# Expert rows turned by VectorE and transfers, second product one tile later, first products before the last routing

## The chip, the core and the metric

The kernel runs on one core of a Trainium2 chip, as one launch. A core has TensorE (PE: matrix products; PEld is its loading of weights), VectorE (DVE), ScalarE (ACT), GpSimd (POOL) and SyncE (SP), which run their instruction queues side by side and wait for one another by semaphores, and 16 DMA engines. The metric is the device time of one execution in microseconds (us). It is given as the median of several runs; a profile is one further execution with the hardware profiler.

## What is computed

The input is 4 sequences of 512 tokens of 512 features, all in f32. Two layers follow, each with an attention-like part and a feed-forward part, both gated and added to the stream. Layer 0 (quantised products with each sequence's own weights, then a ternary feed-forward) and the 16-head cross attention of layer 1 are not touched in what they compute. What the change is about is the last part, a mixture of experts:

```python
router_in = norm_w * (xf * rsqrt(mean(xf * xf) + EPS))
probs = softmax(router_in @ router_w.T)
topw, topi = top_k(probs, 2);  topw = topw / sum(topw)
cw = zeros((T, 8)).at[arange(T)[:, None], topi].add(topw)
a = silu(einsum('td,edf->tef', flat, gate_w)) * einsum('td,edf->tef', flat, up_w)
y = einsum('ted,te->td', einsum('tef,efd->ted', a, down_w), cw) * 4
x = x + tanh(g_ffn[1]) * y        # flat = layernorm(x), 2048 tokens, 8 experts of width 256
```

The kernel computes only the two chosen experts of each token.

## The kernel before, in words

**Attention and what lies beside it.** The 64 heads (16 for each of 4 sequences; LAST is 64) run in a pipelined loop. In one iteration `ask` makes the queries of the next head, `weigh` the scores and softmax of this one (its weights are turned by VectorE in 32x32 blocks, L513, and 16 small transfers, L527, of 64 KB each), `take` multiplies the values of an earlier one (L635) and copies the product to `oT` (ACT, L639), and `add` projects a still earlier one (L649). The last head's 16 transfers are issued from two queues, SP and ACT. A list `beside` holds generators that are advanced by one or two steps an iteration (`step_beside`): the routing of each finished sequence and a sort.

**Routing and sorting.** `route(b)` normalises a sequence, puts its rows (with their eight weights, 520 floats a row) into the table `xtab` in DRAM, and picks two experts for every token (L707 to L790; the products with the router are L748). `sort` gives every token a seat so that the tokens of one expert stand together: 39 tiles of 128 rows, 16 of them (sort a) from the first three sequences, 23 (sort b) from what remains. For each of 24 or 32 columns of tokens it makes one comparison row `in_row` (L905) and two halves of `in_seg` (L907), all on VectorE, and TensorE multiplies them (L912) into the list of row numbers `ids`. Sort b needs the routing of the last sequence, which comes after attention.

**Experts.** The gate and up weights (`gu`) and down weights (`dn`) of all eight experts lie in SBUF. One tile goes through these steps: `gather` (POOL, an indirect transfer of 128 rows, L1021, into one of four buffers `xg`; VectorE picks the tile's weight `cwj`, L1024 and L1025); `expert_in`: four transposes of the rows on TensorE (L1033), a copy to `xgT` by VectorE (L1035), four products with the gate and up weights (L1038; an f32 product runs in two passes, so eight matmuls), Silu on ACT (L1042) and the gating multiply on VectorE (L1043); `expert_out`: two transposes of the hidden values (L1051), a copy to `hidT` (L1053), two products with the down weights (L1056, four matmuls), a copy `y` on ACT (L1060, three buffers), and an indirect scatter-add into the output in DRAM (POOL, L1061). Two tiles may add to one token, so each scatter-add waits until the one before has landed; a dependency written out by hand says so. `expert_out` of a tile is called after `expert_in` of the next one.

**What sets the order.** The program is written in a framework that schedules the instructions of each engine into one fixed order and inserts the waits; pools with a number of buffers decide how far work may run ahead. An engine executes its queue strictly in that order, so an instruction that waits holds all that stands behind it on the same engine, transfers that the engine issues included. In the expert loop gathers run up to three tiles ahead, and from tile 13 on the rest of `beside` (sort b) is run out first.

Of the kernel before, what the change touches and what calls it, by code (L numbers as in the profile page):

```python
# [32 lines left out]
NHEAD, NKV, HD = 16, 8, 128  # L33
# [8 lines left out]
NE, TOPK, FE = 8, 2, 256  # L42
NF = FE // P
# [4 lines left out]
NSEG = (TOK * TOPK + NE * (P - 1)) // P  # L48
NA, TA = 16, 12
NB = NSEG - NA  # L50
ROW = D + NE
# [5 lines left out]
def kernel(  # L57
# [30 lines left out]
    ident = cp.tile([P, P], F32, name="ident")  # L88
# [8 lines left out]
    gu = wp.tile([P, NE, KD, 2 * FE], F32, name="gu")  # L97
    dn = wp.tile([P, NE, NF, D], F32, name="dn")
# [31 lines left out]
    def acc_tile():  # L130
        return acc_p.tile([P, 512], F32, tag="acc", name="acc")
# [68 lines left out]
    with tc.tile_pool(name="q8", bufs=1) as q8, tc.tile_pool(name="l0", bufs=2) as l0, tc.tile_pool(  # L200
        name="w0", bufs=1
# [291 lines left out]
        for b in range(B):  # L493
            xT = ternary_in(b)
# [4 lines left out]
            keys_values(b, lambda: bank(3), load_context(b, nc.sync))  # L499


    l1_ctx = ctx.enter_context(ExitStack())

    la = l1_ctx.enter_context(tc.tile_pool(name="la", bufs=2, reuse_waits="tile"))
    l1 = l1_ctx.enter_context(tc.tile_pool(name="l1", bufs=2, reuse_waits="tile"))

    NQ, Q = P // 32, 32
# [64 lines left out]
        nc.vector.tensor_reduce(seen[b], u8, AX.X, ALU.max)  # L572

    def load_queries(n):
        th = la.tile([P, KD, HD], F32, tag="wq", name="wq")
# [131 lines left out]
    def route(b, pool):  # L707
# [5 lines left out]
        if b + 1 < B:  # L713
            xn, xT, blocks = gu[:, 4], spare_xT if b % 2 == 0 else homes[b], turn_blocks()
        else:
            xn = pool.tile([P, NT, D], F32, name="xnl")
            xT = pool.tile([P, NQ, KD, P], F32, name="xTl")
            blocks = None
        ss = small(NT, "ss")
        for t in range(NT):  # L720
            norm(t, xn[:, t, :D])
            if blocks is not None:
                turn_tile_apart(xn[:, t, :D], blocks, t)
            else:
                tp = work_tile()
                for i in range(KD):
                    nc.tensor.transpose(tp[:, i * P : (i + 1) * P], xn[:, t, i * P : (i + 1) * P], ident)
                evacuate(
                    xT.rearrange("p a k q -> p (a k q)").rearrange("p (q k t) -> p t k q", k=KD, t=NT)[:, t],
                    tp.rearrange("p (k q) -> p k q", k=KD),  # L730
                )
            sq = gu[:, 5, 2 + t % 2, :] if b + 1 < B else pool.tile([P, D], F32, tag="sq", name="sq", bufs=2)
# [12 lines left out]
        for t in range(NT):  # L745
            ps = work_tile()
# [96 lines left out]
    def sort(pool, part, nt, c0, n, spans):  # L843
# [52 lines left out]
        yield  # L896

        if c0:
            in_row = pool.tile([P, TOPK * nt, P], BF16, name="in_row")
        else:  # L900
            in_row = place_in(gu, 5 * SLOT, TOPK * nt * P // 2).bitcast(BF16).rearrange("p (i q) -> p i q", q=P)
        in_seg = pool.tile([P, TOPK * nt, 2, n], BF16, name=part + "in_seg", bufs=1)
        for i in range(TOPK * nt):
            s, t = divmod(i, nt)
            nc.vector.tensor_scalar(in_row[:, i, :], col, lo[:, s, t : t + 1], None, ALU.is_equal)  # L905
            for u, v in enumerate((row1[:, 0:1], float(P * t))):
                nc.vector.tensor_scalar(in_seg[:, i, u, :], cols, hi[:, s, t : t + 1], v, ALU.is_equal, ALU.mult)  # L907
            if i % 8 == 7:
                yield
        ps = work_tile()  # L910
        for i in range(TOPK * nt):
# [65 lines left out]


    loads = {NHEAD + e: [(load_dn, e)] for e in range(NE)}
    for i, e in ((24, 6), (30, 0), (48, 7), (44, 1), (57, 2), (60, 4), (62, 3), (63, 5)):  # L980
        loads[i] = [(load_gu, e)]

    for _ in queries_in(0):
        pass
# [3 lines left out]
    for i in range(LAST + 3):  # L988
        b, n = divmod(i, NHEAD)
        if i == 2:  # L990
            router_constants()
        if n == NHEAD - 6 and b + 1 < B:
            beside.insert(0, queries_in(b + 1))
        if i + 1 < LAST:
            ask(i + 1)
        load_head(i + 2)
        if 2 <= i < LAST + 2:
            wos[i - 2] = load_out((i - 2) % NHEAD)
        if i < LAST:
            weigh(i)  # L1000
        for load, e in loads.get(i, ()):
            load(e)
        if i >= 3:
            add(i - 3)
        if 2 <= i < LAST + 2:
            take(i - 2)
        step_beside()
        if b == B - 1:
            step_beside()
    while beside:  # L1010
        step_beside()


    l1_ctx.close()
    mo = ctx.enter_context(tc.tile_pool(name="moe", bufs=1, reuse_waits="tile"))

    def gather(j):
        ids, _, owned = found[j]
        xg = mo.tile([P, ROW], F32, tag="xg", name="xg", bufs=4)
        table = xtab[: TA * P, :] if j < NA else xtab[:, :]  # L1020
        nc.gpsimd.indirect_dma_start(xg, None, table, bass.IndirectOffsetOnAxis(ap=ids, axis=0))  # L1021
        cwj = small(1, "cwj")
        junk = small(NE, "junk")
        nc.vector.tensor_tensor(junk, xg[:, D:], owned, ALU.mult)  # L1024
        nc.vector.tensor_reduce(cwj, junk, AX.X, ALU.add)  # L1025
        return xg, cwj

    def expert_in(j, xg, cwj):

        e = nc.tensor.value_load(found[j][1], min_val=0, max_val=NE - 1)  # L1030
        tp = work_tile()
        for k in range(KD):
            nc.tensor.transpose(tp[:, k * P : (k + 1) * P], xg[:, k * P : (k + 1) * P], ident)  # L1033
        xgT = mo.tile([P, KD * P], F32, tag="xgT", name="xgT", bufs=2)
        nc.vector.tensor_copy(xgT, tp)  # L1035
        ps = acc_tile()
        for k in range(KD):
            nc.tensor.matmul(  # L1038
                ps, lhsT=xgT[:, k * P : (k + 1) * P], rhs=gu[:, bass.ds(e, 1), k, :], start=(k == 0), stop=(k == KD - 1)
            )  # L1040
        h = mo.tile([P, FE], F32, tag="hid", name="hid", bufs=2)
        nc.scalar.activation(h, ps[:, :FE], AF.Silu)  # L1042
        nc.vector.scalar_tensor_tensor(h, h, cwj, ps[:, FE:], ALU.mult, ALU.mult)  # L1043
        return e, h

    written = []

    def expert_out(j, e, h):
        tp = work_tile()
        for f in range(NF):  # L1050
            nc.tensor.transpose(tp[:, f * P : (f + 1) * P], h[:, f * P : (f + 1) * P], ident)  # L1051
        hT = mo.tile([P, NF * P], F32, tag="hidT", name="hidT", bufs=2)
        nc.vector.tensor_copy(hT, tp[:, : NF * P])  # L1053
        ps = acc_tile()
        for f in range(NF):
            nc.tensor.matmul(  # L1056
                ps, lhsT=hT[:, f * P : (f + 1) * P], rhs=dn[:, bass.ds(e, 1), f, :], start=(f == 0), stop=(f == NF - 1)
            )
        y = mo.tile([P, D], F32, tag="y", name="y", bufs=3)
        nc.scalar.copy(y, ps)  # L1060
        add = nc.gpsimd.indirect_dma_start(  # L1061
            yacc,
            bass.IndirectOffsetOnAxis(ap=found[j][0], axis=0),
            y,
            None,
            bounds_check=TOK - 1,
            oob_is_err=False,
            compute_op=ALU.add,
        )
# [12 lines left out]
    got = {}  # L1082
    pending = None
    for j in range(NSEG):
        if j >= NA - 3:
            while beside:
                step_beside()
        for i in range(j, min(j + 3, NSEG)):
            if i not in got and i in found:
                got[i] = gather(i)  # L1090
        e, h = expert_in(j, *got[j])
        if pending is not None:
            expert_out(*pending)
        pending = (j, e, h)
        step_beside()
    expert_out(*pending)


# [33 lines left out]
```

## Time and profile before

| | |
|---|---|
| runs | 1644.98, 1646.61, 1650.31 us; median 1646.61 us |
| profiled execution | 1646.0 us, span of its records 1644.2 us |
| TensorE | busy 1535.6 us, mean granted clock 0.978 |
| VectorE, ACT, POOL busy | 924.0, 565.8, 442.3 us |
| attention ends, experts begin (first L1033 on TensorE) | 1376.38 us |
| last scatter-add starts | 1638.23 us |
| gather (L1021), mean on POOL | 1.0 us, 35 of them after 1375 us |
| scatter-add (L1061), mean on POOL | 1.58 us, 39 of them |
| scatter-add to its landing, median | 4.8 us |
| moved in 1500 to 1550 us | 80 GB/s; in 1300 to 1350 us (attention) 139 GB/s |

How to read it: a timeline line has the start, the busy time, engine, line, operation and tiles of a run of equal instructions, and in brackets the idle time of the engine just before and the instruction that ended it. In the slices of the page, each digit is the busy share of one fortieth of the span in tenths, and PEclk the clock that TensorE was granted. An issue line of a DMA ends with the median time from issue to landing.

### The profile page before, as it was taken

What the parts mean: (1) busy time and instruction counts of PE and PEld (TensorE: products, weight loads), DVE (VectorE), ACT (ScalarE), POOL (GpSimd) and SP (SyncE); (2) the same over time, 40 slices, a digit from 0 to 9 for tenths busy, and PEclk for the clock granted to TensorE, in tenths of its full rate; (3) what the DMA queues carried; (4) which work ended last, traced back from release to release, by engine and by line L of the source; (5) the groups of instructions that cost most, each with busy time, mean ns of one, the idle gap of its engine ahead of it and who ended that gap; (6) DMA issues with size and microseconds to landing.
All of it is one profiled execution on the core that took longest, in us unless ns stands there. A gap on an engine that the chain in (4) does not pass through costs nothing. (4 is left out here: it accounts for less than half of the span.)

```text
span 1644.2 us, 16560 instructions
## 1 busy us (share of the span) xinstructions
PE 1535.6 (93%) x4524; PEld 771.9 (47%) x4524; DVE 924.0 (56%) x2478; ACT 565.8 (34%) x1180; POOL 442.3 (27%) x549
## 2 busy tenths in 40 slices
PE   4786888999999999999999999999999988999997
PEld 2443655676434444445444445444454434544443
DVE  5567777662155555585665764555768553372221
ACT  2645453633333333352333442333522322211111
POOL 1155433432211113131131130131311102334442
PEclk9898999999999999999999998999999998999999
DMA  8552100113445556576455674575756453444341
GB/s 304 194 184 73 65 20 32 46 52 90 141 137 152 145 135 159 135 202 163 106 160 135 165 190 110 136 184 134 212 149 160 130 144 108 77 79 83 73 79 25
DMA packets 109771, 208.26 MB, mean 127 GB/s; under 512 B 28193, under 2 KB 32289, under 8 KB 109681
## 3 DMA queue, kind: packets, MB, share of 16 engines
q0 software_dynamic: 30896, 88.57, 21.7%
q1 hardware_dynamic: 66960, 96.54, 21.6%
q10 hardware_dynamic: 11824, 22.09, 4.0%
q8 instruction: 39, 0.64, 0.2%
q14 instruction: 52, 0.42, 0.1%
HBM read 98.76 MB, written 35.72 MB: 82 GB/s over the span
## 5 line engine op out<-in xcount | busy, mean ns | idle before, releaser
L615 DVE CUSTOM_DVE_ANT_0 e<-bank,mask_b 128x512 f32<-128x512 f32 x256 | 174.9, 688 | 261.4 <-PE bank L610 261.2
L649 PE MATMUL acc<-wo,oT 128*128 128x512 f32 x512 | 235.5, 603 | 4.1 <-ACT oT L639 4.1
L635 PE MATMUL bank<-eT,v 128*128 128x512 f32 x512 | 230.5, 593 | 2.9 <-DMA eT<-blocks 1.7
L610 PE MATMUL bank<-kT,qT 128*128 128x512 f32 x512 | 232.3, 593 | 0.7 <-ACT dn L458 0.7
L618 ACT ACTIVATE e<-e,nmax 128x512 f32<-128x512 f32 x256 | 184.3, 720 | 95.5 <-DVE nmax L615 88.6
L597 PE MATMUL bank<-gu,wq 128*128 128x512 f32 x384 | 178.3, 601 | 2.3 <-DVE nmax L615 2.3
L513 DVE STREAM_TRANSPOSE blocks<-e 128x512 f32<-128x512 f32 x256 | 158.9, 677 | 21.5 <-DMA eT<-blocks 17.5
L649 PEld LDWEIGHTS acc<-wo,oT 128*128 128x128 f32 x512 | 98.8, 194 | 129.7 <-issue 121.9
L635 PEld LDWEIGHTS bank<-eT,v 128*128 128x128 f32 x512 | 97.1, 190 | 126.0 <-issue 112.0
L610 PEld LDWEIGHTS bank<-kT,qT 128*128 128x128 f32 x512 | 97.0, 190 | 124.8 <-issue 114.5
L1038 PE MATMUL acc<-gu,xgT 128*128 x312 | 143.3, 603 | 4.7 <-issue 3.2
L639 ACT COPY oT<-bank 128x512 f32<-128x512 f32 x64 | 37.4, 584 | 306.7 <-PE bank L635 289.7
L576 POOL DMA_DIRECT2D wq<-in_L_xattn_Wq_dram x64 | 48.5, 757 | 264.0 <-PE bank L597 251.8
L597 PEld LDWEIGHTS bank<-gu,wq 128*128 128x128 f32 x384 | 73.0, 192 | 92.9 <-issue 80.5
L591 POOL DMA_DIRECT2D wo<-in_L_xattn_Wo_dram x64 | 36.8, 575 | 270.3 <-PE acc L649 262.6
L626 DVE TENSOR_SCALAR e<-e,rt 128x512 f32<-128x512 f32 x256 | 108.0, 484 | 2.1
L601 ACT ACTIVATE qT<-bank 128x512 f32<-128x512 f32 x64 | 38.2, 597 | 171.8 <-PE bank L597 166.1
L1038 PEld LDWEIGHTS acc<-gu,xgT 128*128 128x128 f32 x312 | 59.9, 194 | 78.8 <-issue 78.3
L405 PE MATMUL acc<-pjT,hT 128*128 128x512 f32 x320 | 87.2, 402 | 5.7 <-DVE hT L430 5.7
L418 PE MATMUL bank<-xfT,fcT 128*128 128x512 f32 x320 | 87.4, 404 | 0.0
L1056 PE MATMUL acc<-dn,hidT 128*128 x156 | 75.8, 608 | 6.0 <-DVE hidT L1053 5.6
L405 PEld LDWEIGHTS acc<-pjT,hT 128*128 128x128 f32 x320 | 59.2, 188 | 19.4 <-DVE hT L430 7.3
(329 smaller groups left out, 1970.8 us busy)
## 6 DMA issues: line engine op xcount, KB each, us to landing
eT<-blocks SPq DMA_DIRECT2D x1016, 64.0 KB, 2.8
wq<-in_L_xattn_Wq_dram POOLq DMA_DIRECT2D x64, 256.0 KB, 4.1
wo<-in_L_xattn_Wo_dram POOLq DMA_DIRECT2D x64, 256.0 KB, 3.1
kd<-dn SPq DMA_DIRECT2D x32, 256.0 KB, 2.4
vd<-dn SPq DMA_DIRECT2D x32, 256.0 KB, 2.0
kT<-kd POOLq DMA_DIRECT2D x32, 256.0 KB, 3.6
v<-vd POOLq DMA_DIRECT2D x32, 256.0 KB, 4.2
stage<-in_L_ffn_w_fc_dram ACTq DMA_DIRECT2D x20, 256.0 KB, 3.0
```

Of the source, the lines that this page charges most:

```text
L405: nc.tensor.matmul(outs[t], lhsT=h[:, t * P : (t + 1) * P], rhs=pjT[:, j, :], start=(j == 0 and u == 0), stop=(j == NH - 1 and u == 1),)
L418: nc.tensor.matmul(ps, lhsT=fcT[:, i, j * P : (j + 1) * P], rhs=xT[u][:, i, :], start=(u == 0 and i == 0), stop=(u == 1 and i == KD - 1),)
L513: nc.vector.transpose(blocks[:, :, :, t, :].rearrange("p c s r -> p s c r"), src.rearrange("p (s c i) -> p s c i", c=NQ, i=Q))
L597: nc.tensor.matmul(ps, lhsT=th[:, i, :], rhs=xT[:, :, i, :], start=(i == 0), stop=(i == KD - 1))
L610: nc.tensor.matmul(ps, lhsT=qT[:, t * P : (t + 1) * P], rhs=kT, start=True, stop=True)
L615: nc.vector.tensor_tensor_reduce(e, ps, mask_b[b], -1.0, 3.0e38, ALU.add, ALU.min, nmax[:, t : t + 1])
L618: nc.scalar.activation(e, e, AF.Exp, bias=nmax[:, t : t + 1], scale=-1.0, accum_out=total[:, t : t + 1])
L626: nc.vector.tensor_scalar(es[:, t, :], es[:, t, :], rt[:, t : t + 1], None, ALU.mult)
L635: nc.tensor.matmul(ps, lhsT=v[:, s, :], rhs=eT[:, :, s, :], start=(s == 0), stop=(s == NT - 1))
L649: nc.tensor.matmul(sums[b][t], lhsT=oT[:, t * P : (t + 1) * P], rhs=to, start=(n == 0), stop=(n == NHEAD - 1))
L1038: nc.tensor.matmul(ps, lhsT=xgT[:, k * P : (k + 1) * P], rhs=gu[:, bass.ds(e, 1), k, :], start=(k == 0), stop=(k == KD - 1))
L1056: nc.tensor.matmul(ps, lhsT=hT[:, f * P : (f + 1) * P], rhs=dn[:, bass.ds(e, 1), f, :], start=(f == 0), stop=(f == NF - 1))
```

## The change

Rows of tiles 4 to 35 are turned in eight groups of four: VectorE turns 32x32 blocks of the four tiles into one buffer, and SP issues 16 transfers of 64 KB that put the blocks in place; TensorE then reads each tile's rows with a step of 16 floats. Tiles 0 to 3 and 36 to 38 are still turned by TensorE. The hidden values of a tile are turned right after its first product and the second product of the tile before, so that the second product comes one tile later than the turn. Gathers run one group ahead (six buffers), and the second sort is run out before tile 12 (when the rows of tiles 16 to 19 are fetched); `step_beside` is called twice a tile.

```diff
+    def turn_rows(tiles, n):
+        blocks = mo.tile([P, NQ, n * P], F32, tag=f"blocks{n}", name="blocks")
+        dst = mo.tile([P, NQ * n * P], F32, tag=f"turned{n}", name="turned", bufs=2)
+        for t, src in enumerate(tiles):
+            nc.vector.transpose(
+                blocks.rearrange("p c (r s t) -> p t s c r", t=NT, s=n)[:, t],
+                src[:, : n * P].rearrange("p (s c i) -> p s c i", c=NQ, i=Q),
+            )
+        for c in range(NQ):
+            for a in range(NQ):
+                nc.sync.dma_start(
+                    dst[c * Q : (c + 1) * Q, a * n * P : (a + 1) * n * P], blocks[a * Q : (a + 1) * Q, c]
+                )
+        return [[dst[:, k * NT + t :: n * NT] for k in range(n)] for t in range(NT)]
...
+    fetch(groups[0])
+    for j in groups[0]:
+        hide(j)
+    for n, group in enumerate(groups):
+        if n + 1 < len(groups):
+            if groups[n + 1][-1] >= NA:
+                while beside:
+                    step_beside()
+            fetch(groups[n + 1])
+        for j in group:
+            hide(j)
+            if waiting:
+                expert_out(*waiting.pop(0))
+            turn_hidden(j)
+            step_beside()
+            step_beside()
+    expert_out(*waiting.pop(0))
```

`fetch` gathers a group and calls `turn_rows`, `hide` is the first product with Silu and gating, `turn_hidden` the turn of the hidden values, and `expert_out` now only the second product, `y` and the scatter-add.

The rows of tiles 0 and 1 are gathered when the last head has been weighed, and their first products run in the last two iterations of the attention loop; those of tiles 2 and 3 come before the routing of the last sequence on TensorE.

```diff
+        if i == LAST:
+            while beside:
+                step_beside()
+            for j in range(len(first_hid)):
+                first_rows[j] = gather(j, la.tile([P, ROW], F32, tag="wq", name="xg"))
+        if i > LAST:
+            start_tile(i - LAST - 1)
```

In both sorts, one half of `in_seg` is made by POOL (L909 after the change), and the generator yields every four columns instead of eight.

```diff
-                nc.vector.tensor_scalar(in_seg[:, i, u, :], cols, hi[:, s, t : t + 1], v, ALU.is_equal, ALU.mult)
-            if i % 8 == 7:
+                (nc.gpsimd if u else nc.vector).tensor_scalar(in_seg[:, i, u, :], cols, hi[:, s, t : t + 1], v, ALU.is_equal, ALU.mult)
+            if i % 4 == 3:
```

Four of the eight gate/up loads move by one to three heads, (57, 2), (60, 4), (62, 3), (63, 5) becoming (55, 2), (58, 4), (61, 5), (62, 3), and some buffers share a tag (`xTl` with `in_row`, `sq` with `xgT`, the query weights with the rows of tiles 0 and 1). In the changed file the lines are: gather L989, its weights L992 and L993, first product L1001, Silu L1002, gating L1003, transposes on TensorE L1015 (tiles 0, 1) and L1079, stream transposes L1065, their transfers L1071, second product L1119, scatter-add L1124.

More of the change, by code (lines that the diff above doesn't have):

```diff
@@ L499 @@
             keys_values(b, lambda: bank(3), load_context(b, nc.sync))
+    keep = ctx.enter_context(tc.tile_pool(name="keep", bufs=1, reuse_waits="tile"))
     l1_ctx = ctx.enter_context(ExitStack())
@@ L574, in load_queries @@
     def load_queries(n):
-        th = la.tile([P, KD, HD], F32, tag="wq", name="wq")
+        th = la.tile([P, ROW], F32, tag="wq", name="wq")
+        th = th[:, : KD * HD].rearrange("p (k n) -> p k n", k=KD)
         nc.gpsimd.dma_start(th, wq[:, n * HD : (n + 1) * HD].rearrange("(k p) n -> p k n", p=P))
@@ L716, in route @@
             xn = pool.tile([P, NT, D], F32, name="xnl")
-            xT = pool.tile([P, NQ, KD, P], F32, name="xTl")
+            xT = pool.tile([P, NQ, KD, P], F32, tag="xTl", name="xTl")
             blocks = None
@@ L731, in route @@
                 )
-            sq = gu[:, 5, 2 + t % 2, :] if b + 1 < B else pool.tile([P, D], F32, tag="sq", name="sq", bufs=2)
+            sq = gu[:, 5, 2 + t % 2, :] if b + 1 < B else pool.tile([P, D], F32, tag="xgT", name="sq", bufs=2)
             nc.scalar.activation(sq, xn[:, t, :D], AF.Square, accum_out=ss[:, t : t + 1])
@@ L898, in sort @@
         if c0:
-            in_row = pool.tile([P, TOPK * nt, P], BF16, name="in_row")
+            in_row = pool.tile([P, TOPK * nt, P], BF16, tag="xTl", name="in_row")
         else:
@@ L979, with gather, expert_in, start_tile @@
     loads = {NHEAD + e: [(load_dn, e)] for e in range(NE)}
-    for i, e in ((24, 6), (30, 0), (48, 7), (44, 1), (57, 2), (60, 4), (62, 3), (63, 5)):
+    for i, e in ((24, 6), (30, 0), (48, 7), (44, 1), (55, 2), (58, 4), (61, 5), (62, 3)):
         loads[i] = [(load_gu, e)]
+    def gather(j, xg):
+        ids, _, owned = found[j]
+        table = xtab[: TA * P, :] if j < NA else xtab[:, :]
+        nc.gpsimd.indirect_dma_start(xg, None, table, bass.IndirectOffsetOnAxis(ap=ids, axis=0))
+        cwj = sm.tile([P, 1], F32, tag="cwj", name="cwj", bufs=10)
+        junk = small(NE, "junk")
+        nc.vector.tensor_tensor(junk, xg[:, D:], owned, ALU.mult)
+        nc.vector.tensor_reduce(cwj, junk, AX.X, ALU.add)
+        return xg, cwj
+    def expert_in(j, cwj, xgT, h):
+        e = nc.tensor.value_load(found[j][1], min_val=0, max_val=NE - 1)
+        ps = work_tile() if j < len(first_hid) else acc_tile()
+        for k in range(KD):
+            nc.tensor.matmul(ps, lhsT=xgT[k], rhs=gu[:, bass.ds(e, 1), k, :], start=(k == 0), stop=(k == KD - 1))
+        nc.scalar.activation(h, ps[:, :FE], AF.Silu)
+        nc.vector.scalar_tensor_tensor(h, h, cwj, ps[:, FE:], ALU.mult, ALU.mult)
+        return e, h
+    first_hid = [keep.tile([P, FE], F32, name=f"hid{j}") for j in range(2)]
+    hidden, first = {}, {}
+    first_rows = {}
+    def start_tile(j):
+        xg, cwj = first_rows.pop(j)
+        tp = work_tile()
+        for k in range(KD):
+            nc.tensor.transpose(tp[:, k * P : (k + 1) * P], xg[:, k * P : (k + 1) * P], ident)
+        xgT = la.tile([P, S], F32, tag="kT", name="xgT")
+        nc.vector.tensor_copy(xgT, tp)
+        first[j] = expert_in(j, cwj, [xgT[:, k * P : (k + 1) * P] for k in range(KD)], first_hid[j])
     for _ in queries_in(0):
@@ L1009 @@
             step_beside()
-    while beside:
-        step_beside()
     l1_ctx.close()
     mo = ctx.enter_context(tc.tile_pool(name="moe", bufs=1, reuse_waits="tile"))
[L1017 to L1026, printed above, removed]
@@ L1028, in expert_in @@
-    def expert_in(j, xg, cwj):
-        e = nc.tensor.value_load(found[j][1], min_val=0, max_val=NE - 1)
-        tp = work_tile()
[L1032 to L1044, printed above, removed]
@@ L1046 @@
-    written = []
[L1048 to L1053, printed above, removed]
+    def turn_rows(tiles, n):
[12 more added lines that the diff above has]
+        return [[dst[:, k * NT + t :: n * NT] for k in range(n)] for t in range(NT)]
@@ new lines, in turn_by_tensor @@
+    def turn_by_tensor(src, n, dst):
+        tp = work_tile()
+        for k in range(n):
+            nc.tensor.transpose(tp[:, k * P : (k + 1) * P], src[:, k * P : (k + 1) * P], ident)
+        nc.vector.tensor_copy(dst, tp[:, : n * P])
+        return [dst[:, k * P : (k + 1) * P] for k in range(n)]
+    rest = list(range(NT, NSEG - NSEG % NT))
+    groups = [list(range(NT))] + [rest[i : i + NT] for i in range(0, len(rest), NT)]
+    groups.append(list(range(NSEG - NSEG % NT, NSEG)))
+    turned_in = {}
@@ new lines, with fetch, turn_in @@
+    got = {}
+    def fetch(group):
+        for j in group:
+            if j not in got:
+                got[j] = gather(j, mo.tile([P, ROW], F32, tag="xg", name="xg", bufs=6))
+        if group not in (groups[0], groups[-1]):
+            for j, t in zip(group, turn_rows([got[j][0] for j in group], KD)):
+                turned_in[j] = t
+    def turn_in(j):
+        if j not in turned_in:
+            dst = mo.tile([P, KD * P], F32, tag="xgT", name="xgT", bufs=2)
+            turned_in[j] = turn_by_tensor(got[j][0], KD, dst)
+        return turned_in.pop(j)
@@ L1054, in expert_out, with hide, turn_hidden @@
+    def hide(j):
+        if j not in hidden:
+            h = mo.tile([P, FE], F32, tag="hid", name="hid", bufs=3)
+            hidden[j] = expert_in(j, got[j][1], turn_in(j), h)
+    def turn_hidden(j):
+        e, h = hidden[j]
+        hT = turn_by_tensor(h, NF, mo.tile([P, NF * P], F32, tag="hidT", name="hidT", bufs=2))
+        waiting.append((j, e, hT))
+    written = []
+    def expert_out(j, e, hT):
         ps = acc_tile()
@@ L1056, in expert_out @@
             nc.tensor.matmul(
-                ps, lhsT=hT[:, f * P : (f + 1) * P], rhs=dn[:, bass.ds(e, 1), f, :], start=(f == 0), stop=(f == NF - 1)
+                ps, lhsT=hT[f], rhs=dn[:, bass.ds(e, 1), f, :], start=(f == 0), stop=(f == NF - 1)
             )
@@ L1081 @@
     beside += [route(B - 1, mo), sort(mo, "b", TT, NA, NB, other_tiles)]
[L1082 to L1096, printed above, removed]
+    hidden.update(first)
+    got.update((j, None) for j in first)
+    waiting = []
+    fetch(groups[0])
[7 more added lines that the diff above has]
+            fetch(groups[n + 1])
+        for j in group:
+            hide(j)
[5 more added lines that the diff above has]
+    expert_out(*waiting.pop(0))
 _INS = [
```

## The prediction

> **What bounds the kernel now.** I began with the busy row and the slices of the page.
>
> ```profile
> PE 1535.6 (93%) x4524; PEld 771.9 (47%) x4524; DVE 924.0 (56%) x2478; ACT 565.8 (34%) x1180; POOL 442.3 (27%) x549
> PE   4786888999999999999999999999999988999997
> PEclk9898999999999999999999998999999998999999
> ```
>
> TensorE is the bound in nearly every slice; the soft slices are the beginning, which the diff leaves alone, and slices 33 and 34 (about 1356 to 1438 us), where attention hands over to the experts. All edits lie from 1318 us on, so I read the rest there. TensorE's timeline of the steady expert stage shows one period:
>
> ```profile
> 1521.77 3.60 PE L1038 MATMUL acc<-gu,xgT 128*128 x8
> 1525.20 0.38 PE L1051 MATMUL bank<-ident,hid 128*128 128x128 f32 x2
> 1525.42 0.60 PE L1033 MATMUL bank<-ident,xg 128*128 128x128 f32 x4
> 1526.19 1.95 PE L1056 MATMUL acc<-dn,hidT 128*128 x4 [0.17 <-DVE hidT L1053]
> 1527.98 3.60 PE L1038 MATMUL acc<-gu,xgT 128*128 x8
> ```
>
> From start to start: 3.43 first product, 0.22 hidden turns, 0.77 row turns (0.17 of it waiting for the hidT copy that the turns cover), 1.79 second product: 6.21 us a tile, 39 tiles. The handover, in the same view:
>
> ```profile
> 1351.64 1.96 PE L635 MATMUL bank<-eT,v 128*128 128x512 f32 x4 [1.68 <-DMA eT<-blocks]
> 1356.92 6.45 PE L649 MATMUL acc<-wo,oT 128*128 128x512 f32 x8 [3.32 <-ACT oT L639]
> ...
> 1376.38 1.06 PE L1033 MATMUL bank<-ident,xg 128*128 128x128 f32 x8
> 1380.67 9.94 PE L1038 MATMUL acc<-gu,xgT 128*128 x16 [3.23 <-issue]
> ```
>
> Three idles (1.68, 3.32, 3.23 us). After the two long ones the same matmuls run slowly: L649 x8 takes 6.45 against 3.70 later (granted clock 0.57 in 1355 to 1360), and 16 L1038 take 9.94 against 2 x 3.43. The short idle cost nothing more.
>
> Last, POOL's timeline and the DMA landings of the page, because each scatter-add (L1061) waits for the landing of the one before:
>
> ```profile
> 1434.70 1.61 POOL L1061 DMA_INDIRECT out_dram<-y,aids  x1 [0.30 <-issue]
> 1440.52 1.55 POOL L1061 DMA_INDIRECT out_dram<-y,aids  x1 [4.21 <-DMA out_dram<-y,aids]
> ```
> ```profile
> 1616.12 1.55 POOL L1061 DMA_INDIRECT out_dram<-y,bids  x1 [4.66 <-ACT y L1060]
> 1622.34 1.55 POOL L1061 DMA_INDIRECT out_dram<-y,bids  x1 [4.67 <-ACT y L1060]
> ```
> ```profile
> eT<-blocks SPq DMA_DIRECT2D x1016, 64.0 KB, 2.8
> out_dram<-y,bids POOLq DMA_INDIRECT x23, 4.8
> ```
>
> A scatter-add lands 4.85 us after its start, and the next began 0.75 us after such a landing. The chain's shortest pitch is thus 5.6 us (5.82 in the first pair). TensorE's 6.21 hides it: in the second pair POOL waits for y. The margin is 0.6 us a tile.
>
> **Part by part.**
>
> *Row turns leave TensorE.* For tiles 4 to 35 the four L1033 go, 0.77 us each: 32 x 0.77 = 24.6 us. The period becomes 3.43 + 1.79 + 0.22 = 5.44. The second product one tile later puts 3.43 us of first product in place of the turns as cover for the hidT copy (0.42); Silu and the gating multiply (0.38 + 0.47) lie beside the 1.79 of the second product. The strided weight reads of the turned rows have a near row: L748 loads with the same stride, 0.308 us each against 0.194 for L1038, and still less than the 0.43 between matmuls. Cost 0; at worst, if nothing of a load were hidden, 8 x 0.11 = 0.9 a tile; I take 0.
>
> *What supplies the turned rows.* Per group of four: 4 stream transposes (L513: 0.677 each, 2.7) in place of 4 copies (L1035: 0.682), even on VectorE, and 16 SP transfers, issued 0.63 us apart (10.1), landing after 2.8. Latency 2.7 + 10.1 + 2.8 = about 16 us, against 4 x 5.44 = 21.8 us of TensorE. VectorE's next transposes wait for these 16 (blocks has one buffer); by the built order only the next group's gating stands behind them, and 16 is less than 21.8, so hidden: 0. A rule speaks against this. The Trainium skill ("VectorE: DVE Perf Modes", "The three transpose paths") warns that a plain DMA with strides as a transpose is 19 times slower than the DMA transpose, given at 1.309 us for 128x128 bf16. An estimate from it, 25 us for one such block, would put a group at 38 us or more: 8 x 16 = some 130 us lost. The row decides: 1016 transfers of this form and size landed at 2.8, because the 32x32 turning is done by VectorE and each piece moves whole runs. I take the row.
>
> *Early tiles 0 and 1.* Their first products and turns, 2 x (3.43 + 0.45) = 7.8 us, now stand between the last heads' products on TensorE. They can fill the 1.68 and 3.32 idles and spare 2.9 of slow clock. ACT's eight transfers ahead of the oT copy stay, so the wait stays; only its cover is new. Worth 5 to 8, and the 3.23 idle with its slow stretch stays (tiles 2 and 3 still wait for VectorE, busy with the last norm).
>
> *Sort.* 32 of the 64 seat comparisons of sort b go to POOL (L909). POOL showed none at 23 columns: L375 at 512 and 256 columns took 1.55 and, at its least, 0.92 us, which extrapolates to 0.35; bounds 0.175 (its smallest CAST) and 0.92. I take 0.35: 11.2 us (5.6 to 29). VectorE saves 32 x 0.2 = 6, off the path. In the built order all 32 stand between scatter-adds 4 and 5 on POOL, so scatter-add 5 and the gathers for tiles 16 on queue behind them. Behind those, VectorE's weight product (L992) of tile 16 stands ahead of tile 10's gating (L1003): TensorE waits there some 6 to 9 us, plus about 2.9 of slow clock. A smaller wait of that kind at tile 4 (L992 of tiles 14, 15): 2.6. Sort a's 24 lie in the attention stage, where POOL has room: 0.
>
> *Gathers.* They are still 39, 1.0 us + 0.3 each, but now four in a row before a group. After a scatter-add (1.6) four gathers take 5.2, so the next starts at 7.1 instead of 5.6: 1.5 more for each of five groups, and 3.8 where six stand together: 11.3 in all. Six row buffers for four, the shared tags and the order of the gate/up loads: 0, since no wait for them stands at the handover of before; a load that came late there would cost its lateness once, a few us at most by their landings of 6.3 and 7.4.
>
> **The sums.** The profiled execution took 1646.0, span 1644.2 and 1.8 around it; the median of the runs is 1646.61, as good as the same.
>
> TensorE alone: 1644.2 - 24.6 - 6.5 + 2.6 + 7.5 + 2.9 = 1626, or about 1615 if the tile-10 wait is caught up or smaller.
>
> Scatter-add chain: the first starts where it did (1395.6), as its y does. Four pitches of 5.6 and two gathers bring number 4 to about 1420; its 1.6 and 11.2 of L909 put number 5 at 1432.6 (1434.7 before). Then 31 pitches to number 36 = 173.6, gathers 11.3, and two short ones for the nearly empty last tiles (landing 2.7, pitch 3.5) = 7: number 38 starts at 1624.5, lands 2.7 later, and as before 3.3 us pass to the end: 1630.5; time 1632.3. That is later than TensorE, y has only three buffers, and a blocked ACT stops TensorE within three tiles. So **the new bound is the chain**: 5.44 of TensorE against 5.6 + 1.5/4 = 6.0 of POOL. Most of the 25 us turns into waiting for scatter-adds.
>
> **Rivals.**
>
> 1. *The chain binds as summed*: 1632, between 1625 and 1641 for a pitch of 5.35 to 5.9. For it: the 4.21 us wait for a landing above. Against: only a few such pitches were seen in before. 0.5.
>
> 2. *TensorE stays the bound*: gathers overlap landings better or L909 costs 0.175, and the time is 1615 to 1625. Against: needs a pitch near 5.2. 0.13.
>
> 3. *Slower: the chain lengthens under the SP transfers.* They add 1 MB per 21.8 us, 48 GB/s, to some 80, on the same 16 DMA engines as the scatter-adds. One scatter-add of before, near the handover, landed after 5.73: a pitch of 6.5 gives 31 x 0.9 = 28 more, 1660. It decides from a pitch of 5.6 + 19.2/31 = 6.2, which is before's whole period. The Trainium skill ("SBUF — State Buffer", "SBUF: two separate sides") names a further way: a VectorE operation in a two-port mode locks POOL out of writing descriptors, so its DMAs start late. By the row the stream transposes run at 512 columns in 677 ns, one element a cycle of the page's 0.96 GHz, so I count 0; by the rule each could hold one scatter-add up to 0.7 us, 4 x 8 x 0.7 = 22 at most. For it: the load is new beside a serial chain. Against: attention ran at 139 GB/s and its landings stayed 2 to 4. L909 at 0.92 (+18, 1650) works to the same side. 0.25 for slower, 0.12 for something between.
>
> 4. *The turned rows come late* (a group above 21.8 us): each us over costs 8; contained in 3's chance.
>
> **How the numbers follow.** Predicted 1632. Rival 1 and 2 are faster, with a little of 1's upper end in the middle: faster 0.63, same 0.12 (1641.7 to 1651.5: 0.3% is about what a measurement of this kernel can tell from no change), slower 0.25. The range takes in rival 2's bound and the lower half of rival 3: 1615 to 1656, leaving out some 0.05 below and 0.13 above. The chain's own range is 1625 to 1641.
>
> **What would show it.** Right: the row-turn group shrinks to 28 of 156; L1061's idle is ended mostly by DMA out_dram, not by ACT y; its starts lie 5.6 to 6 apart with one longer step in four; TensorE has many short idles, at second products or for free banks; turned transfers land 8 us ahead of use. Wrong: POOL still waits for y (TensorE bound, rival 2); L1119 or L1001 wait for turned (rival 4); landings above 5.5 (rival 3); L909 above 0.6 us each. If the handover still shows 3.3 us idle before the last heads' projection, the early tiles bought nothing, and 5 to 8 us are missing from TensorE's sum, though not from the chain's.

## The result, and the profile after

The changed kernel takes 1655.94 us (median of 7 runs, 1653.47 to 1658.1) against 1646.61 for the kernel before: ratio 1.0053, 95% interval 1.0041 to 1.0066. It is slower by 9 us, where 1632 was predicted. It lies at the very edge of the stated range of 1615 to 1656. The upper part of that range stood for scatter-adds delayed by the new transfers, which is not what happened, so it is luck that the range just holds the result. Its profiled execution took 1653.89 us with a span of 1652.1, so all that follows is read from a run at the low end of these.

The page of the changed kernel, the same rows as before:

```profile
PE 1524.4 (92%) x4388; PEld 783.4 (47%) x4396; DVE 929.0 (56%) x2422; ACT 566.5 (34%) x1180; POOL 465.4 (28%) x605
PE   4786888899999999999999999999999999968997
PEclk9899999999999999999999998999999999989999
```

TensorE does 11 us less work in 8 us more time. The soft slices have moved: no longer 33 and 34 (1315 to 1398 us; the prediction's 1356 to 1438 is one slice too late), but 36 and, less, 37 (1446 to 1528 us), in the middle of the experts, with a lower clock in slice 36.

TensorE's timeline at the handover:

```profile
1351.70 3.70 PE L1001 MATMUL bank<-gu,xgT 128*128 x8 [1.20 <-DVE xgT L1017]
...
1357.82 3.60 PE L651 MATMUL acc<-wo,oT 128*128 128x512 f32 x8
...
1377.20 1.04 PE L1079 MATMUL bank<-ident,xg 128*128 128x128 f32 x8
1380.92 8.61 PE L1001 MATMUL acc<-gu,xgT 128*128 x16 [2.68 <-DVE xgT L1080]
```

The idles of 1.68 and 3.32 us before the last heads' products are gone, and the clock no longer falls there: the last heads' projection (now L651) takes 3.60 us instead of 6.45, and the granted clock is 1.00 in 1355 to 1360. The first products of tiles 0 and 1 lie in their place: attention ends at 1377, as before (1376.4), with two tiles' products done. The idle before tiles 2 and 3 stays (2.68, was 3.23).

The same view in the expert stage, one undisturbed tile and one group's disturbance:

```profile
1462.28 0.69 PE L1079 MATMUL bank<-ident,hid 128*128 128x128 f32 x2 [11.91 <-DVE hid L1003]
...
1509.79 1.88 PE L1119 MATMUL acc<-dn,hidT 128*128 x4
1516.62 0.44 PE L1079 MATMUL bank<-ident,hid 128*128 128x128 f32 x2 [4.95 <-DVE hid L1003]
1517.44 5.18 PE L1001 MATMUL acc<-gu,turned 128*128 x8 [0.38 <-issue]
1522.46 1.88 PE L1119 MATMUL acc<-dn,hidT 128*128 x4
...
1525.09 3.78 PE L1001 MATMUL acc<-gu,turned 128*128 x8 [0.53 <-DMA turned<-blocks]
...
1530.64 3.80 PE L1001 MATMUL acc<-gu,turned 128*128 x8
1534.28 1.88 PE L1119 MATMUL acc<-dn,hidT 128*128 x4
1536.00 0.38 PE L1079 MATMUL bank<-ident,hid 128*128 128x128 f32 x2
1536.22 3.80 PE L1001 MATMUL acc<-gu,turned 128*128 x8
```

An undisturbed tile takes 5.58 us (1530.64 to 1536.22). But TensorE stands 11.91 us at tile 10 and 4.95 us at tile 18, both times at the turn of hidden values that VectorE has not gated yet, and after the second the first product runs in 5.18 instead of 3.80 (granted clock 0.79 in 1516 to 1524). VectorE's timeline says what it did meanwhile:

```profile
1461.48 0.17 DVE L992 TENSOR_TENSOR junk<-xg,bowned 128x8 f32<-128x8 f32 x1 [14.25 <-DMA xg<-xtab,bids]
1461.68 0.16 DVE L993 TENSOR_REDUCE cwj<-junk 128x1 f32<-128x8 f32 x1
1461.76 0.47 DVE L1003 SCALAR_TENSOR_TENSOR hid<-hid,cwj,acc 128x256 f32<-128x256 f32 x1
...
1506.69 3.65 DVE L1065 STREAM_TRANSPOSE blocks<-xg 128x512 f32<-128x512 f32 x4
1516.01 0.17 DVE L992 TENSOR_TENSOR junk<-xg,bowned 128x8 f32<-128x8 f32 x1 [5.67 <-DMA xg<-xtab,bids]
1516.09 0.48 DVE L1003 SCALAR_TENSOR_TENSOR hid<-hid,cwj,acc 128x256 f32<-128x256 f32 x1
```

It was idle, waiting for a gather to land. L992 (called the pick below) takes a tile's weight out of gathered rows; the rows are those of a tile that TensorE needs six tiles later at tile 10 and twelve at tile 18, but in VectorE's fixed order the pick stands ahead of the gating L1003 of the tile that TensorE waits for now. POOL's timeline shows why the gather is late:

```profile
1423.23 15.06 POOL L909 TENSOR_SCALAR bin_seg<-col,bhi 128x23 bf16<-128x23 f32 x32
1438.56 1.59 POOL L1124 DMA_INDIRECT out_dram<-y,aids  x1 [0.27 <-ACT y L1123]
...
1455.42 1.56 POOL L1124 DMA_INDIRECT out_dram<-y,aids  x1 [3.81 <-DMA out_dram<-y,aids]
1457.28 1.04 POOL L989 DMA_INDIRECT xg<-xtab,bids  x1 [0.30 <-issue]
...
1509.91 1.56 POOL L1124 DMA_INDIRECT out_dram<-y,bids  x1 [3.97 <-DMA out_dram<-y,aids]
1511.77 1.02 POOL L989 DMA_INDIRECT xg<-xtab,bids  x1 [0.30 <-issue]
...
1516.89 1.63 POOL L1124 DMA_INDIRECT out_dram<-y,bids  x1 [0.31 <-issue]
1525.28 1.57 POOL L1124 DMA_INDIRECT out_dram<-y,bids  x1 [6.77 <-ACT y L1123]
```

The comparisons hold POOL for 15.06 us. Scatter-add 5 (1438.56) starts 11.3 us after its `y` was ready, three more follow, each after the landing of the one before, and only then comes the gather of tile 16, at 1457.28, for which the pick ahead of tile 10's gating waits. Later it is the same without the comparisons: the gather of 1511.77 stands behind a scatter-add that waited 3.97 us for the landing of the one before; four gathers follow in a row; and then the next scatter-add but one waits 6.77 us for a `y` that could not be made, because TensorE stood. It is a loop through four engines: scatter-add, gather, pick, gating, `y`, scatter-add.

Laid side by side by the starts of the second products (L1056 before, L1119 after; worked out from the two traces), the changed kernel is 7.4 us ahead at tile 9, loses 14.0 at tile 10, and ends 8.0 behind at tile 38. In between, tiles 11 to 35 gain 25 x 0.63 = 15.8 us by the shorter period, but lie 20.2 us above that period in sum, where the kernel before lay 3.1 above its own. Tiles 18, 22 and 26, where a pick holds a gating, have 13.3 of the 20.2. A smaller part is a wait of 0.5 to 0.8 us for turned rows before the first product of tiles 16, 20, 24 and 28, one in each group (1525.09 above).

### The profile page after: what moved, and what is told of

Same layout as the page of the kernel before. It is cut to its first block, busy times and chain, and to the rows that moved or that the text cites. A ratio compares the mean times of both kernels' runs of the same rounds, so it can differ in the third digit from the quotient of the medians.

```text
span 1652.1 us, 16451 instructions
## 1 busy us (share of the span) xinstructions
PE 1524.4 (92%) x4388; PEld 783.4 (47%) x4396; DVE 929.0 (56%) x2422; ACT 566.5 (34%) x1180; POOL 465.4 (28%) x605
## 3 DMA queue, kind: packets, MB, share of 16 engines
q1 hardware_dynamic: 73104, 104.94, 23.2%
## 5 line engine op out<-in xcount | busy, mean ns | idle before, releaser
L651 PE MATMUL acc<-wo,oT 128*128 128x512 f32 x512 | 232.6, 596 | 0.3 <-ACT oT L641 0.3
L651 PEld LDWEIGHTS acc<-wo,oT 128*128 128x128 f32 x512 | 97.7, 191 | 123.3 <-issue 120.6
L1001 PE MATMUL acc<-gu,turned 128*128 x256 | 125.8, 633 | 3.9 <-DMA turned<-blocks 2.4
L1001 PEld LDWEIGHTS acc<-gu,turned 128*128 128x128 f32 x256 | 73.5, 299 | 37.1 <-issue 9.9
L1119 PE MATMUL acc<-dn,hidT 128*128 x156 | 75.4, 607 | 2.1 <-DVE hidT L1080 2.1
L429 POOL TENSOR_TENSOR r<-r 128x512 f32<-128x512 f32 x40 | 42.4, 1061 | 93.9 <-ACT hT L428 93.9
```

The source lines that it names most:

```text
L651: nc.tensor.matmul(sums[b][t], lhsT=oT[:, t * P : (t + 1) * P], rhs=to, start=(n == 0), stop=(n == NHEAD - 1))
L1001: nc.tensor.matmul(ps, lhsT=xgT[k], rhs=gu[:, bass.ds(e, 1), k, :], start=(k == 0), stop=(k == KD - 1))
L1119: nc.tensor.matmul(ps, lhsT=hT[f], rhs=dn[:, bass.ds(e, 1), f, :], start=(f == 0), stop=(f == NF - 1))
```

## The experiments

Theory A: VectorE's queue is the cause; a pick that waits for a gather holds the gating behind it. Theory B: the scatter-add chain sets the time, as the prediction had it, and the waits for `hid` are only where its lateness shows. Theory C: the turned rows, their reads or their transfers cost.

**Picks behind the gatings.** A dependency without a semaphore, on VectorE's order alone (`gated[j]` is the gating of tile j):

```diff
-        nc.vector.tensor_tensor(junk, xg[:, D:], owned, ALU.mult)
+        pick = nc.vector.tensor_tensor(junk, xg[:, D:], owned, ALU.mult)
+        if j >= 14:
+            tc.add_manual_dep(pick.ins, gated[5 if j < 16 else 11 if j < 22 else j - 10].ins.name, ...)
```

> The changed kernel, with one order imposed on VectorE: the weight pick of a gathered tile (L992) stands behind the gating of tile 5 (tiles 14, 15), of tile 11 (16 to 21) or of the tile ten before its own, instead of ahead of them; nothing else is moved by hand. Theory A (VectorE's queue: a pick that waits for a gather holds the gating behind it, and TensorE waits for that gating): the waits of L1079 for hid (11.9 us at tile 10, 4.95, 2.1 and 1.2 later) go, with their slow stretches some 30 us of TensorE; then the scatter-add chain is next: number 5 at 1438.6, 31 pitches of 5.5, 11 for gathers, 7 and 6 at the end, time about 1636 (1630 to 1642). Theory B (the scatter-add chain sets the time already, the waits for hid are only where its lateness shows): the idle moves to banks or to y and the time stays within 4 us of 1656. Theory C (turned rows come late from SP): L1001 waits for turned longer, 1650 or more.

1640.55 us, ratio to before 0.9951 (0.9929 to 0.9972): 15 us less than the changed kernel, so B in its plain form falls, and the time lies in A's range. What is left is in tiles 10 to 14, which take 35.3 us there against 21.9 in the kernel with both edits below: the stream transposes of tiles 16 to 19 (L1074 in this kernel) now wait for the late gathers, ahead of a gating.

```profile
1471.33 1.89 DVE L1074 STREAM_TRANSPOSE blocks<-xg 128x512 f32<-128x512 f32 x2 [11.56 <-DMA xg<-xtab,bids]
```

**Seats on VectorE.**

```diff
-                (nc.gpsimd if u else nc.vector).tensor_scalar(in_seg[:, i, u, :], ...)
+                nc.vector.tensor_scalar(in_seg[:, i, u, :], ...)
```

> The changed kernel with the seat comparisons of both sorts back on VectorE; the rest stays. The 32 on POOL took 15.1 us between scatter-adds 4 and 5. Theory A: scatter-add 5 starts some 15 us earlier and the gathers behind it too, so the wait at tile 10 shrinks from 11.9 us to 0 to 5; the waits in the later groups (4.95, 2.1, 1.2) stay, as they have nothing to do with the sort: about 1643 (1638 to 1648). Theory B: the whole chain is 15 us earlier and so is the end: 1641. A third (sort b is bound by VectorE and its steps, not by POOL): list of rows as late as before, 1654 to 1658.

1654.72, 1.0042 (1.0028 to 1.0056): A missed, and so did B. The third theory has the number but not the reason: the gather of tile 16 did come earlier, at 1452.33 instead of 1457.28. Scatter-add 5 started 5.8 us earlier and not 15. Tiles 6 to 10 took 25.8 us instead of 37.6, but 10 to 26 took 115 instead of 107: most of the 12 us won at tile 10 was given back, and the trace shows picks waiting ahead of gatings in the later groups (4.4, 2.0, 2.0 and 1.3 us of TensorE).

**Both.**

> Both edits: picks behind the gating, and the seat comparisons on VectorE. Theory A: both waits gone; TensorE at 5.6 us a tile and the scatter-add chain at 5.5 and 1.5 per group of gathers run side by side: 1622 to 1630, faster than before. Theory B: as with the comparisons on VectorE alone, 1641. Theory C: not better than the better of the two alone.

1631.30, 0.9917 (0.9890 to 0.9943): faster than both kernels, just above A's bound. TensorE's idle time before L1079 (here L1088) that the gating ended fell from 23.4 us to 2.2. What binds now is seen in POOL's timeline of this kernel:

```profile
1506.08 1.63 POOL L1133 DMA_INDIRECT out_dram<-y,bids  x1 [0.30 <-issue]
1513.06 1.58 POOL L1133 DMA_INDIRECT out_dram<-y,bids  x1 [5.35 <-DMA out_dram<-y,bids]
1518.64 1.56 POOL L1133 DMA_INDIRECT out_dram<-y,bids  x1 [4.00 <-DMA out_dram<-y,bids]
...
1582.10 1.55 POOL L1133 DMA_INDIRECT out_dram<-y,bids  x1 [3.96 <-DMA out_dram<-y,bids]
1587.63 1.55 POOL L1133 DMA_INDIRECT out_dram<-y,bids  x1 [3.98 <-DMA out_dram<-y,bids]
```

Scatter-adds follow one another 5.5 us apart, 7.0 where a group's gathers stand near, and wait for landings: the picture that the prediction drew. From scatter-add 11 on, each `y` lay ready 2.8 to 12.0 us before its scatter-add started, and where no gathers stand between, the start came 0.74 to 0.80 us after the landing of the one before, wherever the trace has that landing. From scatter-add 5 to 36 the chain took 186.8 us, against 184.9 in the prediction's sum.

**Only the picks of the second sort (tiles 14 to 21).** The condition above is `14 <= j < 22`, seats on POOL.

> The changed kernel with only the picks of tiles 14 to 21 put behind the gatings of tiles 5 and 11; all later picks stay where the change has them, and the seats stay on POOL. Theory A: the 14 us at tile 10 go, the waits of the later groups (some 18 in all) stay or grow, since POOL is no further: between the changed kernel and the one with all picks moved (1640), about 1646 to 1654. If the wait at tile 10 was the whole loss: about 1640.

1656.90, 1.0041 (1.0025 to 1.0056): as the changed kernel, a little above A's 1646 to 1654. Tiles 6 to 10 fell to 23.9 us, but 10 to 14 rose to 37.1, where stream transposes wait 10.6 us for the same gathers. One wait of this kind taken away is found again here at the next instruction of VectorE that needs the gather.

**Rows by TensorE again.** `turn_rows` is never called; the rest of the change stays.

```diff
-        if group not in (groups[0], groups[-1]):
+        if False:
```

> The changed kernel with all rows turned by TensorE again (no stream transposes, no SP transfers for them); second product one tile later, early products, seats on POOL, six row buffers and calls for a group stay. Theory A: gathers come free tile by tile again, so no pick waits long in the steady stage; TensorE's period is 6.2 again, which covers the scatter-add chain; what is left is the gain of the early tiles (7) against a wait at the second sort: 1640 to 1650. Theory C (the strided reads and the transfers are what costs): faster than 1642. If the early tiles and the seats are what costs: above 1655.

1686.42, 1.0238 (1.0207 to 1.0269), which no theory gave. VectorE's timeline has the cause, A's own, which I had thought gone:

```profile
1530.40 0.17 DVE L992 TENSOR_TENSOR junk<-xg,bowned 128x8 f32<-128x8 f32 x1 [5.24 <-DMA xg<-xtab,bids]
...
1531.36 0.47 DVE L1003 SCALAR_TENSOR_TENSOR hid<-hid,cwj,acc 128x256 f32<-128x256 f32 x1
```

The scheduler put two picks ahead of a gating for every second tile: 28.3 to 28.9 us per four tiles in most of the stage instead of 24.9 before, some 20 us in tiles 10 to 38. Another 15 were lost by tile 10, most of them in a wait of 10.34 us at tile 7, where a pick stood ahead of a gating while POOL worked on the comparisons. To test it, the same kernel with each pick behind the gating of the tile two before (called from `hide`), and seats on VectorE:

> Rows turned by TensorE as in the kernel with only that undone (1686), but seats on VectorE and each pick behind the gating of the tile two before. Theory A (picks ahead of gatings made that kernel slow): the 1.6 to 1.9 us waits for hid before every second tile and the slow start go, TensorE's 6.21 us a tile is the bound again: 32 tiles at 0.6 more than with the turned rows, about 1640 to 1648, 40 us better than 1686. If transposes or calls for a group themselves were slow: above 1670.

1644.97, 0.9980 (0.9962 to 0.9997): A, and 41 us less. The order of the picks and the place of the comparisons were not taken apart here; four tiles in the steady stage now take 24.6 us instead of 28.3 to 28.9, and there the picks are what changed.

It also gives a rough price of the turned rows: 1644.97 - 1631.30 = 13.7 us. The two kernels were measured at different times, each beside runs of the kernel before; by the ratios to those the difference is 10 us, give or take 5. Part of it is an idle of TensorE of 5.96 us before the first product of tile 7 in the kernel with rows on TensorE, whose cause the trace doesn't name. In the steady stage TensorE takes 23.0 us for four tiles with turned rows and 24.6 without: 0.4 us a tile.

**Without the chain.** The scatter-add is replaced, and the experts' part is left out of the output:

```diff
-        add = nc.gpsimd.indirect_dma_start(yacc, ..., y, None, ..., compute_op=ALU.add)
+        nc.gpsimd.dma_start(apart[j * P : (j + 1) * P], y)
```

> As the kernel with picks behind the gating and seats on VectorE (1631), but y is stored to rows of its own in DRAM by a plain POOL transfer, so no store waits for the landing of another; what is left out is adding the experts' part to the output. Theory A with the chain as the next bound: it falls to TensorE's own sum, 5.6 us a tile without lag: 1618 to 1626. If the chain was no bound there: 1629 to 1633.

1625.67, 0.9861 (0.9826 to 0.9896): the chain is worth 5.6 us in the kernel with both edits (9 by the ratios, give or take 7, since these two were also measured at different times). In the traces, TensorE keeps 22.7 to 23.2 us for four tiles from tile 18 to 34 with and without the chain. What the chain costs is 2.2 us in tiles 14 to 18 and 4.5 after the last second product, where its scatter-adds still have to land one after the other.

> As the one without the chain, and TensorE reads the turned rows as 128 neighbouring columns instead of with a step of 16 (the products then take rows in a wrong order: the computed values are left wrong, amounts and shapes stay). If the step costs the 0.14 to 0.2 us a tile by which the period is above 5.44: 32 x 0.17 = 5 less than without the chain. If loads are hidden as predicted: the same within 1.

1625.73, 0.9857 (0.9823 to 0.9891): no difference. The loads of turned rows in the groups of the kernel with both edits, and of this one:

```profile
L1010 PEld LDWEIGHTS acc<-gu,turned 128*128 128x128 f32 x256 | 73.2, 298 | 32.5 <-issue 5.0 <-ACT y L1132 2.6
```
```profile
L1010 PEld LDWEIGHTS acc<-gu,turned 128*128 128x128 f32 x256 | 46.2, 191 | 50.5 <-issue 49.8 <-ACT y L1133 0.7
```

A load of neighbouring columns takes 191 ns instead of 298, and the period stays at 5.56 to 5.58: loads lie beside the matmuls. Of C, the reads fall with this one; the transfers keep the 0.5 to 0.8 us that the first product of a group waits for them.

> The changed kernel with nothing else edited but the scatter-adds, replaced by plain stores as above (the experts' part is not added to the output). Picks still stand ahead of gatings. Theory A in its full form (a pick waits because its gather stands on POOL behind scatter-adds that wait for landings): gathers are issued as soon as buffers are free, the waits for hid mostly vanish: 1620 to 1632. If the pick waits come from the row buffers or from y alone: still 1640 or more.

1634.01, 0.9911 (0.9883 to 0.9938): just above A's range, 22 us below the changed kernel. With the same order on VectorE, but gathers no longer behind stores that wait for landings, the wait at tile 10 shrinks to 1.00 us and all waits for `hid` together to 7.0. So it takes both to make the loss: the pick ahead of the gating, and a gather behind a slow chain.

**Without the early tiles** (`first_hid` empty, on top of both edits):

> As the kernel with picks behind the gating and seats on VectorE (1631), but tiles 0 and 1 are gathered and multiplied after attention with the others; the early products are gone. By the prediction's sum they are worth 5 to 8 us on TensorE, but not to the scatter-add chain, whose first start hardly depends on them. If the chain alone sets the time: 1630 to 1634. If TensorE still counts in the first stage: 1636 to 1640.

1636.27, 0.9914 (0.9882 to 0.9946): 5.0 us more, but measured at another time than the 1631.30, and the ratios (0.9914 and 0.9917) don't tell the two apart. In the traces the second products come 8.5 us later at tile 6 and 7.8 at tile 38, of which 0.8 was there before the edit acts. The chain isn't indifferent either: its scatter-add 5 starts at 1434.7 instead of 1427.4.

**Gathers spread** (on top of both edits: from tile 24 on, each gather behind the scatter-add nine tiles earlier, again by an order on POOL alone):

> As the kernel with picks behind the gating and seats on VectorE (1631), but from tile 24 on the gathers are no longer four in a row: one stands behind each scatter-add on POOL, eight tiles ahead. If the chain with its 1.4 us per group of gathers sets the time, four groups fewer are worth 4 to 6: 1625 to 1628. If TensorE sets it: 1630 to 1632. If a stream transpose now waits for a late gather ahead of a gating: above 1634.

1676.36, 1.0173 (1.0140 to 1.0205): the third case, and a blunder of mine that shows the loop best. VectorE and POOL of this kernel:

```profile
1565.76 0.17 DVE L999 TENSOR_TENSOR junk<-xg,bowned 128x8 f32<-128x8 f32 x1 [7.81 <-DMA xg<-xtab,bids]
```
```profile
1558.21 1.57 POOL L1143 DMA_INDIRECT out_dram<-y,bids  x1 [8.50 <-ACT y L1142]
1560.09 1.01 POOL L989 DMA_INDIRECT xg<-xtab,bids  x1 [0.30 <-issue]
```

The gather now follows a scatter-add that waits for `y`; the pick waits for the gather; the gating, and with it the next `y`, wait for the pick. Four tiles take 34 us instead of 23.

## Why the prediction was wrong, step by step

*The step that failed* is the sentence "by the built order only the next group's gating stands behind them" together with the part on gathers, which charged them to POOL's chain alone, 1.5 us a group. The order that I had read places a pick ahead of a gating of the current group in nearly every group; I followed it at tiles 4 and 10 and not further. It is a wait of TensorE: 2.2 us at tile 4 (I had 2.6), 14.0 at tile 10 (I had 9 to 12) and 13.3 at tiles 18, 22 and 26 (I had none). Putting the picks behind took 15 us off, removing the comparisons from POOL besides 9 more.

The way of summing failed with it. I added up TensorE and the chain apart and let the later one decide, but here each delays the other. In the changed kernel scatter-adds 5 to 36 took 197 us where my sum had 185, as from 18 on nearly all waited for a `y` that TensorE made late.

*Right only after the repair:* the chain as the next bound. Its pitch of 5.5 to 5.7, and 7.0 with gathers, was predicted at 5.6 and 7.1, and in the kernel with both edits it ends last. That this kernel's 1631.3 lies beside the predicted 1632 is luck in part, since 11.2 us of the predicted sum are comparisons on POOL, which it doesn't have; the kernel that has them, with the picks behind, took 1640.55. In the kernel as changed the chain is not what ends last. The sign that the prediction named speaks against it there; the waits of the changed kernel:

```profile
POOL out_dram L1124 <- ACT y L1123: 100.7, 23, 6.9
POOL out_dram L1124 <- DMA out_dram<-y,aids: 31.0, 7, 5.7
```

From scatter-add 18 on, all but three start 0.27 or 0.28 us after their own `y` is made.

*Right in size:* strided reads at 0. The early tiles were put at 5 to 8, and the changed kernel is 7.4 us ahead at tile 9; the times of the runs don't settle it, and their effect on the chain's start was missed.

*Mis-sized:* the period, 5.58 instead of 5.44. The strided reads are not its reason (5.56 without); what is stays open. The supply of turned rows was to be hidden, landing 8 us ahead of use; the first product of four groups waited 0.5 to 0.8 us for it, 2.4 in all, and a stream transpose into this layout took 1.02 us where 0.677 stood in the nearest row. A comparison on POOL took 15.06 / 32 = 0.47 us, against 0.35. The turned rows were summed at 0.77 us a tile, 24.6 in all; the steady stage gives 0.4 a tile. The longer period takes 0.14 of the difference, and the tile with the wait for turned rows, 6.0 to 6.3 us once in four, some 0.15.

*The rival that was slower* had the right side and the wrong cause. The trace of the changed kernel holds no landings, but in the others scatter-adds did not land later beside the SP transfers; the DMA issues of the kernel with both edits, which has these transfers:

```profile
turned<-blocks SPq DMA_DIRECT2D x128, 64.0 KB, 3.9
xg<-xtab,bids POOLq DMA_INDIRECT x23, 5.7
out_dram<-y,bids POOLq DMA_INDIRECT x23, 4.8
```

4.8 us, as before. What landed later are the gathers, 5.7 instead of 3.4, which makes a pick behind them wait longer. The rule on strided transposes of the Trainium skill ("VectorE: DVE Perf Modes", "The three transpose paths") is stated for a large innermost stride at the destination. These transfers move whole runs, and 64 KB landed in 3.9 us (2.8 for the like ones before), so the estimate made from the rule does not apply to them; a transfer that turns single elements was not run. And no run shows the lock of the skill's "SBUF — State Buffer" ("SBUF: two separate sides") lengthening a scatter-add: with the stream transposes, one holds POOL for 1.55 to 1.63 us, as before. (The prediction's "one element a cycle" for those is loose: at the 0.96 GHz that it takes from the page, 512 elements would be 533 ns and not 677.)

*Open:* why the kernels with one wait repaired (seats alone; picks of the second sort alone) return to within 2 us of the changed one. The traces show where the time goes, not that it must come out equal. Whether a schedule that puts picks on another engine would do as well was not tried.

## What to carry to other kernels

When work is fetched further ahead, list every instruction that touches the fetched data, down to one of 0.17 us, and ask for each queue what stands behind it: a prefetch moves a wait into an in-order queue long before the data is needed. In a loop of queues (store, fetch, small use, gating, product, store) like this one, a wait repaired in one place came back in another (the seats alone, the picks of the second sort alone), so look at the order on all of them, and read it from the built program for the whole stage and not for its first case. Two sums that end close together may not be taken apart when each queue waits for the other. An order imposed between two instructions of one engine needs no semaphore and was worth 15 us and, in another variant, 41 together with one more edit.

## What the runs showed of the hardware that was not expected

In the changed kernel an idle of 1.16 us on TensorE (1570.15) left the first product after it at 3.80 us, and 1.68 us in the kernel before had cost nothing either; but after 2.13 us (1543.87) it took 5.22, as long as after 4.95. The kernel with rows on TensorE narrows this: eight idles of 1.58 to 1.88 us left the next first product at 3.60, and one of 2.14 (1487.60) was followed by 5.29. But length alone does not decide: with the seats on VectorE alone, 1.28 and then 0.35 us (1569.11) were followed by 5.50 us, at a granted clock of 0.76 in 1569 to 1576. What else does, no run shows.

A gather that lands after 3.4 us when issued singly landed after 5.7 (median) when issued in fours beside the SP transfers, while scatter-adds on the same queue kept their 4.8. Which of the two, the fours or the transfers, makes it later was not separated.
